# Gates for three batches at a time, alternating half signs and a padded third layer in the mixing stage of a fused transformer block

## The chip, the cores and the metric

The kernel runs on one core of one Trainium2 chip. It is written in Bass and Tile: a Python program emits instructions for the engines PE (TensorE, matrix products), ACT (ScalarE, activations), DVE (VectorE), POOL (GpSimd) and SP (SyncE, which here only issues transfers). Each engine works through its own queue in order, and engines wait for one another by semaphores. The metric is the device time of one execution in microseconds (us). Before the change three runs took 1777.57, 1782.65 and 1783.18 us; their median is 1782.65.

## The reference

The input `x` is 8 batches of 256 rows of 256 features in fp32. Three blocks follow one another, each with a residual and a layer norm behind it:

1. `x = LN(x + attn(x))`: six layers of causal linear attention (16 heads) and a feed-forward net, 256 to 1024 to 256.
2. `x = LN(x + xattn(x, ctx))`: differential cross attention. Each of 16 heads has two softmaxes, from two pairs of projections, and the second is subtracted with a weight `gain`. The heads' outputs are normalized and multiplied by `wo`.
3. `x = LN(x + ffn(x))`: the mixing stage, which the change is mostly about:

```python
gf = _global_net(x.mean(axis=1, keepdims=True))      # 256 -> 128 -> 64 -> 1, one number per batch
out = x
for _ in range(3):                                    # the three cycles
    tf = _coupling_net(out)                           # 256 -> 256 -> 128 -> 64 -> 1, one number per row
    combined = 0.7 * gf + 0.3 * tf
    coupling = 0.1 + adaptive_range * (combined - 0.5) * 2.0
    out = out + coupling * _twist(out)
return out
```

`_twist` splits a row into four quarters `o_r, o_i, p_r, p_i` and returns `[p_r, -p_i, -o_r, o_i]`. Both nets use the exact gelu between their layers and a sigmoid at the end, which the kernel computes as a tanh of half the argument.

## The kernel before, in words

All eight batches stay in the core's memory, a batch as two tiles of 128 rows by 256 features (`xr[b]`). The program is a list of tasks, one per batch and stage (`stage_q`, `stage_s`, `stage_w`, `stage_f` for the attention layers; `setup_u`, `stage_u`, `stage_u2`, `stage_xo` for cross attention; `stage_pre`, `stage_ff` for mixing). Each task is a generator that yields due times, and `run_tasks` always resumes the task that is due first (`NOW[0]` is the due time that it has reached). So the order in which instructions are emitted is a plan made of due times. On PE that order is kept by force: `mm` and `tp` (a product, and a transpose as a product with the identity, all under lines 138 and 143) chain each instruction behind the one before it. `table_op` does the same for those ACT instructions that need a function table (exp, gelu, tanh). Every other instruction is placed in its engine's queue by the scheduler, which follows emission order but lets an instruction whose operands come earlier go first.

Products accumulate in PSUM banks, which are handed out in turn from the pools `p_q` (four), `p_h` (two), `p_o` (one) and `p_av` (one). In cross attention `PU(kind)` picks the pool by the kind of work, in the mixing stage `PF()` goes round `q h q q h q o`.

**Cross attention, about 1383 to 1652 us.** It consists of 32 passes: eight batches, two halves of the heads, two halves of each half. `stage_u` makes the scores once for their row maxima (L836, tile `nm`), and these maxima ride along in the second scores product, which `stage_u2` makes: eight products, each followed by an exp on ACT (L867, whose outputs lie in the buffers `a`, `wraw`, `hl` and `avs`). Sixteen narrow products with the values then sum into `p_av`. ACT copies that to memory (L878, `qe`), PE transposes the copy (`p_h<-ident,qe`, L143), DVE divides by the row sums (L887 to L892, `rc` and `o`) and POOL subtracts the two softmaxes (L894, `fo`). Emission interleaves passes: the products and exps of the next pass are emitted between a pass's `p_av` and its transposes. After every fourth pass `stage_xo` normalizes the heads' outputs (square on ACT L905), transposes them, copies them on ACT (L920, `hl`), multiplies by `wo` (`p_h<-w2h,hl`), adds to the residual (DVE, L928) and normalizes (`normalize2`, whose last step on ACT is L338).

**The mixing stage, about 1653 to 1776 us.** `start_ff` negates one quarter of each batch. Three batches have a head start in `stage_pre`, late in cross attention. `stage_ff(b, cyc)` then runs for three cycles of eight batches, due `FFP` = 3.1 apart; the offsets `F_O` are the due times inside it. A batch of a cycle is: four transposes; a cast on ACT (L1050, `wah`) and the rest on DVE (L1055, `wal`), which split the fp32 value into two parts of the reduced type fp32r; a first layer of 256 by 256 as three fp32r products per tile (`mm3`: high times high, high times low, low times high); two gelus (L1066, `hf`); a split on DVE and POOL (L1076, L1077, `hh` and `hl`); a second layer to 128; a gelu (L1089); a split (L1098 on DVE, L1099 on POOL or DVE); a third layer to 64 columns, three fp32r products; a gelu (L1108); a fourth layer to one number (`f_w,a`, 64 rows deep); a tanh (L1124, `cp`); two activations that make the coefficients for the two halves, with opposite signs (L1126); and four updates on DVE, two per row tile (L1134). In cycle 2 the first layer is split, the second and third are single fp32 products on unsplit weights (tile `num`) and values. Cycle 2 ends with the residual, the last normalization and the store.

In cycle 0 a batch also computes its gate, alone: row sums by DVE (L1003, `osm` in `stage_pre`, `gsum` in `stage_ff`), four products with the first gate weight (`osm,rb` or `gsum,rb`, one column), gelu (L1072), a product to 64, gelu, a product of the broadcast weight, tanh (L1113) and two `base` activations (L1116). The weights of the mixing stage are loaded and split by `prep_mix`, whose work falls into cross attention; `prep_ffn` loads the small ones early.

Of the kernel before, what the change touches and what calls it, by code (L numbers as in the profile page):

```python
# [52 lines left out]
FFP = 3.1  # L53
F_O = (1.45, 2.0, 2.85, 7.6, 11.4, 14.5)
# [39 lines left out]
def decoder_kernel(ctx: ExitStack, tc: tile.TileContext, A, out, nlay=NLAY, groups=GROUPS):  # L94
# [8 lines left out]
    def C(name, shape, dt=F32):  # L103
        return cpool.tile(list(shape), dt, name=name)
# [625 lines left out]
    def PU(kind):  # L730

        if kind == "v":
            return PS("av")
        if NOW[0] < T_END:
            return PS("q")
        if kind == "1":
            return PS("qqo"[turn("1", 3)])
        return PS("q" if kind == "2" else "h")

    wide = []  # L740
# [110 lines left out]
    def stage_u2(b, c, hh, u):  # L851

        tq, tk = stq[u % SD], stk[u % SD]
        if u % 4 == 0:
            xst[b]["oc"] = T2("fo", 2)
        oc = xst[b]["oc"]
        va = xst[b][c][2]
        es = []
        for k in range(2):
            for h in range(4):  # L860
                t = (4 * k + h) * UH / 8
                yield us(t)
                ps = PU("2")
                mm(flat(ps), lhsT=tk[0:98, h, half(k)], rhs=flat(tq[0:98, 2 * h:2 * h + 2, :]), start=True, stop=True)
                yield us(t + 0.5)
                e = ET()
                table_op(act.activation(e, ps, AF.Exp))  # L867
                es.append(e)
        yield us(t + U_O[1])
        po = PU("v")  # L870
        for k in range(2):
            for h in range(4):
                mm(flat(po[32 * h:32 * h + 32]), lhsT=va[:, k, 4 * hh + h, :], rhs=flat(es[4 * k + h]),
                   start=k == 0, stop=k == 1, tile_position=(0, 32 * h))
        t += U_O[1]
        yield us(t + 1.4)
        ov = T2("qe", 2)
        act.copy(ov, po)  # L878
        yield us(t + 2.2)
        pt = PU("x")  # L880
        for mp in range(2):
            for s in range(2):
                tp(pt[:, mp, half(s)], ov[:, mp, half(s)], ident)
        yield us(t + 2.9)
        p5 = pt.rearrange("p m (s h n) -> p m s h n", s=2, h=4)
        rc = S("rc", [P, 2, 2, 4], bufs=2)
        dve.reciprocal(rc, p5[:, :, :, :, 16])  # L887
        dve.tensor_scalar(rc[:, 1], rc[:, 1], gain, None, ALU.mult)
        c0 = (8 * c + 4 * hh) * 16
        og = oc[:, :, c0:c0 + 64].rearrange("p s (h n) -> p s h n", h=4)  # L890
        o2 = S("o2", [P, 2, 2, 4, 16], bufs=2)
        dve.tensor_tensor(o2.rearrange("p m s h n -> p (m s) h n"), p5[:, :, :, :, 0:16].rearrange("p m s h n -> p (m s) h n"),  # L892
                          rc.rearrange("p m s h -> p (m s) h").unsqueeze(3).to_broadcast([P, 4, 4, 16]), ALU.mult)
        pool.tensor_tensor(og, o2[:, 0], o2[:, 1], ALU.subtract)  # L894

    def stage_xo(b, X_O):
# [23 lines left out]
        act.copy(oT, pt)  # L920
# [13 lines left out]
    def prep_ffn():  # L934
        def keep(nm, shape, src, parts=P):
            t = C("f_" + nm, [P] + shape)
            load(t[0:parts], src)
            FW[nm] = t[0:parts]
# [4 lines left out]
        keep("w4", [1], A["L0_ffn_cn_w4"], 64)  # L943
# [4 lines left out]
        keep("cb3", [1], col(A["L0_ffn_cn_b3"]), 64)  # L948
# [6 lines left out]
        ars = C("f_ars", [P, 6])  # L955
        for i, x in enumerate((0.3, -0.3, 0.7, -0.7)):
            dve.tensor_scalar(ars[:, i:i + 1], FW["ar"], x, None, ALU.mult)
        pool.memset(ars[:, 4:5], 0.1)
        pool.memset(ars[:, 5:6], -0.1)
        FW["ars"] = ars  # L960

    def prep_mix():

        raw = [T2("hf", 3), T2("num", 1, F32R).bitcast(F32)]
        sp.dma_start(out=raw[0], in_=A["L0_ffn_cn_w1"].rearrange("(k p) n -> p k n", p=P))
        r2 = raw[1][:, :, 0:P]
        r3 = raw[1][:, 0, P:P + 64]
        sp.dma_start(out=r2, in_=A["L0_ffn_cn_w2"].rearrange("(k p) n -> p k n", p=P))
        sp.dma_start(out=r3, in_=A["L0_ffn_cn_w3"])
# [6 lines left out]
        h2, l2 = T2("xTh", 2, F32R), T2("xTl", 2, F32R)  # L976
        yield 1.1
        for h, x in ((hi, raw[0]), (h2[:, :, 0:P], r2), (h2[:, 0, P:P + 64], r3)):
            dve.tensor_copy(h, x)
        yield 1.2  # L980
        for l, h, x in ((lo, hi, raw[0]), (l2[:, :, 0:P], h2[:, :, 0:P], r2), (l2[:, 0, P:P + 64], h2[:, 0, P:P + 64], r3)):
            pool.tensor_tensor(l, x, h, ALU.subtract)
        FW.update(c1=(hi, lo), c2=(h2[:, :, 0:P], l2[:, :, 0:P]), c3=(h2[:, 0, P:P + 64], l2[:, 0, P:P + 64]), g1=g1, r2=r2, r3=r3)
# [6 lines left out]
    def first_layer(xh, xl, ps):  # L990

        ch, cl = FW["c1"]
        for m in range(2):
            mm3(ps[m], [(ch[:, c, half(m)], cl[:, c, half(m)]) for c in range(2)], [(xh[:, c, :], xl[:, c, :]) for c in range(2)])
            yield m
# [6 lines left out]
    def feature_sums(pt, sm):  # L1002
        dve.tensor_reduce(sm, pt, AX.X, ALU.add)  # L1003
        return sm

    def stage_pre(b, deep):
# [11 lines left out]
        if "sums" not in FW:  # L1018
            FW["sums"] = S("osm", [P, 16], bufs=1)
        i = order.index(b)  # L1020
        sm = feature_sums(pt, FW["sums"][:, 2 * i:2 * i + 2])
# [7 lines left out]
        fst[b]["pre"] = (xh, xl, sm, ps)  # L1029

    def stage_ff(b, cyc):
# [8 lines left out]
        if pre:  # L1040
            xh, xl, sm, ps = pre
        else:
# [8 lines left out]
            if cyc == 2:  # L1051
                pool.tensor_tensor(xr[b], xr[b], o, ALU.add)
                d["xo"] = xr[b]
            yield us(F_O[1])
            dve.tensor_tensor(xl, pt, xh, ALU.subtract)  # L1055
            if cyc == 0:
                sm = feature_sums(pt, S("gsum", [P, 2], bufs=2))
# [6 lines left out]
        for m in range(2) if done else first_layer(xh, xl, ps):  # L1064
            yield us(F_O[2] + 0.7 + 0.7 * m)
            table_op(act.activation(hf[:, m, :], ps[m], AF.Gelu, bias=FW["cb1"][:, m:m + 1]))  # L1066
        if cyc == 0:
            pg = PF()
            for c in range(2):
                mm(pg[:, 0, 0:1], lhsT=FW["g1"][:, c, :], rhs=sm[:, c:c + 1], start=c == 0, stop=c == 1)  # L1070
            g1 = S("gg1", [P, 1], bufs=3)
            table_op(act.activation(g1, pg[:, 0, 0:1], AF.Gelu, bias=FW["gb1"], scale=1.0 / 256))  # L1072
# [7 lines left out]
        if cyc < 2:  # L1080
            ch, cl = FW["c2"]
            mm3(ps[:, 0, :], [(ch[:, c, :], cl[:, c, :]) for c in range(2)], [(hh[:, c, :], hl[:, c, :]) for c in range(2)])
        else:
            for c in range(2):
                mm(ps[:, 0, :], lhsT=FW["r2"][:, c, :], rhs=hf[:, c, :], start=c == 0, stop=c == 1)
# [4 lines left out]
        if cyc == 0:  # L1090
            pg = PF()
            mm(pg[0:64, 0, 0:1], lhsT=FW["g2"], rhs=g1, start=True, stop=True)
            g2 = S("gg2", [64, 1], bufs=3)
            table_op(act.activation(g2, pg[0:64, 0, 0:1], AF.Gelu, bias=FW["gb2"]))
        yield us(F_O[3] + 1.2)
        if cyc < 2:
            hs = T2("hh", HHB, F32R)
            dve.tensor_copy(hs[:, 0, :], h2)  # L1098
            (dve if pre else pool).tensor_tensor(hs[:, 1, :], h2, hs[:, 0, :], ALU.subtract)  # L1099
        yield us(F_O[4])  # L1100
        ps = PF()
        if cyc < 2:
            mm3(ps[0:64, 0, :], [FW["c3"]], [(hs[:, 0, :], hs[:, 1, :])])
        else:
            mm(ps[0:64, 0, :], lhsT=FW["r3"], rhs=h2, start=True, stop=True)
        yield us(F_O[4] + 0.4)
        h3 = h23[0:64, 1, :]
        table_op(act.activation(h3, ps[0:64, 0, :], AF.Gelu, bias=FW["cb3"]))  # L1108
        if cyc == 0:
            pg = PF()  # L1110
            mm(pg[:, 0, 0:1], lhsT=g2.to_broadcast([64, P]), rhs=FW["g3"], start=True, stop=True)
            gt = S("gt", [P, 1], bufs=2)
            table_op(act.activation(gt, pg[:, 0, 0:1], AF.Tanh, bias=FW["gb3"], scale=0.5))  # L1113
            base = S("base", [P, 2], bufs=8)
            for q in range(2):
                act.activation(base[:, q:q + 1], gt, AF.Identity, bias=FW["ars"][:, 4 + q:5 + q], scale=FW["ars"][:, 2 + q:3 + q])  # L1116
            d["base"] = base
# [7 lines left out]
        for q in (1, 0):  # L1125
            act.activation(cp[:, 2 * q:2 * q + 2], cp[:, 0:2], AF.Identity, bias=d["base"][:, q:q + 1], scale=FW["ars"][:, q:q + 1])  # L1126
# [5 lines left out]
        for t in range(2):  # L1132
            for q in range(2):
                dve.scalar_tensor_tensor(no[:, t, half(q)], o[:, t, half(1 - q)], cp[:, 2 * q + t:2 * q + t + 1], base_o[:, t, half(q)], ALU.mult, ALU.add)  # L1134
        d["o"] = no
        if cyc == 2:
            y = no
            yield us(F_O[5] + 2.2)
            dve.tensor_scalar(y[:, :, q1], y[:, :, q1], -1.0, None, ALU.mult)
# [36 lines left out]
    for i, b in enumerate(order):  # L1176
# [13 lines left out]
        tasks.append((t_end + us(UH + U_XO), 1.0, lambda b=b, i=i: stage_xo(b, X_O[i == len(order) - 1])))  # L1190
    t_f = t_u + us(U_FF)
    for i, t in enumerate((18.0, 11.0, 4.0)):
        tasks.append((t_u - us(t), 1.0, lambda b=order[i], deep=i < 2: stage_pre(b, deep)))
    tasks.append((t_f - 2.9, 1.0, prep_mix))
    for cyc in range(3):
# [64 lines left out]
```

## Time and profile before

The profile is of one execution of the program, which took 1778.4 us by itself, with a span of 1776.6 us and a mean granted PE clock of 0.986.

| stage | from to (us) | length | PE busy | DVE busy | ACT busy |
|---|---|---|---|---|---|
| cross attention | 1383 to 1652 | 269 | 249.24 | 228.16 | 213.74 |
| head of mixing | 1652 to 1664 | 12 | 9.14 | 7.09 | 6.06 |
| cycle 0 | 1664 to 1707 | 43 | 42.89 | 28.33 | 33.68 |
| cycle 1 | 1707 to 1732 | 25 | 24.47 | 24.30 | 21.41 |
| cycle 2 | 1732 to 1760 | 28 | 28.00 | 19.22 | 24.32 |
| tail | 1760 to 1776.6 | 16.6 | 4.59 | 9.21 | 9.87 |

Over the whole span PE is busy for 1697.5 us (96%), DVE for 1292.3, ACT for 1173.5 and POOL for 824.7. The borders of the stages are read from PE's products; neighbouring stages overlap on the other engines.

A line of the timeline gives the start in us, the duration in us, the engine, the line of the program, the operation, output and inputs by the program's tile names, shapes, and how many equal instructions it stands for. What stands in brackets is the idle time of the engine before it and what ended that time. A line of the windows gives, after the stretch and its length, the busy time of PE, of PE's weight loads, of DVE, ACT and POOL, each with the number of instructions in brackets, then the granted clock, the busy share of the transfer engines and their GB/s.

### The profile page before, as it was taken

To read this page: it belongs to the slowest core of one execution; us is meant where nothing else is said; L and a number is where in the kernel's file an instruction comes from. 1 tells how busy PE (TensorE), PEld (TensorE's weight loads), DVE (VectorE), ACT (ScalarE), POOL (GpSimd) and SP (SyncE) were. 2 spreads that over 40 slices of the span, in tenths; PEclk is the share of its full clock that TensorE was granted. 3 is DMA by queue.
4 is the path that set the end of the run, shared out by engine and by line. 5 is a ranking of instruction groups with operands and counts; after the bars stand their busy time and mean duration, and the time that the engine had idled before them with its cause. 6 is when DMAs were issued, how large, how long until landed. Compare 5 with 4: busy or idle time off the path is not lost.

```text
span 1776.6 us, 38400 instructions
## 1 busy us (share of the span) xinstructions
PE 1697.5 (96%) x14992; PEld 1352.7 (76%) x14992; DVE 1292.3 (73%) x2855; ACT 1173.5 (66%) x2297; POOL 824.7 (46%) x1289
## 2 busy tenths in 40 slices
PE   6999999999999999999999999999988899999997
PEld 4688887888878888788888887888776645554795
DVE  5566868667776677776787666777668898887586
ACT  3566665666656666667666665666665788887687
POOL 7333444344433444444344434444566676743263
PEclk9899999999999999999999999999999999999898
DMA  5000001000010000100011001000003354440001
GB/s 153 10 1 2 22 19 49 2 1 22 19 49 1 2 22 29 39 1 1 23 37 42 2 1 37 22 22 2 16 25 95 103 145 115 113 126 25 1 1 48
DMA packets 63262, 64.23 MB, mean 36 GB/s; under 512 B 10261, under 2 KB 56600, under 8 KB 63082
## 3 DMA queue, kind: packets, MB, share of 16 engines
q1 hardware_dynamic: 62058, 61.51, 12.2%
q8 instruction: 118, 1.93, 0.4%
q0 software_dynamic: 1024, 0.28, 0.1%
q14 instruction: 62, 0.51, 0.1%
HBM read 49.67 MB, written 11.81 MB: 35 GB/s over the span
## 4 chain that ended last, share of the span: by engine, by line
PE 71%; DVE 13%; ACT 6%; POOL 5%; issue 3%; DMA 1%; SPq 1%; POOLq 0%; ACTq 0%; DVEq 0%
PE p_q L138 24%; PE p_h L138 18%; PE p_o L138 13%; PE p_av L138 10%; PE p_q L143 4%; PE p_h L143 2%; DVE nm L836 2%; DVE a L505 2%; POOL stk L524 1%; POOL hl L579 1%; DVE hh L576 1%; DVE bst L317 1%; POOL nz L295 1%; ACT hf L596 1%; ACT L451 1%
## 5 line engine op out<-in xcount | busy, mean ns | idle before, releaser
L596 ACT ACTIVATE hf<-p_h,bcol 128x256 f32<-128x256 f32 x384 | 161.4, 475 | 214.3 <-PE p_h L138 213.7
L524 POOL TENSOR_SCALAR_AFFINE_SELECT stk<-stk 128x256 f32<-128x256 f32 x384 | 172.6, 475 | 238.4 <-ACT stk L521 235.1
L579 POOL TENSOR_TENSOR hl<-hf,hh 128x512 fp32r<-128x512 f32 x144 | 195.2, 1356 | 160.7 <-DVE hh L576 132.3
L138 PE MATMUL p_q<-stq,kf 32*128 32x512 f32 (+2 forms) x1664 | 248.7, 521 | 10.2 <-ACT wraw L867 1.9
L521 ACT COPY stk<-p_q 128x512 f32<-128x512 f32 x384 | 198.7, 599 | 84.9 <-PE p_q L138 84.4
L294 POOL TENSOR_SCALAR nv<-bmv 128x2 f32<-128x2 f32 x128 | 34.2, 267 | 324.8 <-DVE bmv L319 307.9
L138 PEld LDWEIGHTS p_o<-w2h,hh 128*128 128x128 f32 x768 | 117.8, 190 | 73.3 <-issue 71.9
L138 PE MATMUL p_h<-xTh,w1h 128*128 128x256 f32 x768 | 168.1, 300 | 1.3 <-DVE xTl L392 1.0
L138 PE MATMUL p_o<-w2h,hh 128*128 128x256 f32 x768 | 167.8, 300 | 0.8 <-DVE xr L614 0.8
L138 PE MATMUL p_h<-xTl,w1h 128*128 128x256 f32 x768 | 154.8, 283 | 0.7 <-DVE xTl L392 0.7
L138 PE MATMUL p_h<-xTh,w1l 128*128 128x256 f32 x768 | 154.6, 283 | 0.0
L138 PE MATMUL p_o<-w2h,hl 128*128 128x256 f32 x768 | 152.1, 279 | 0.0
L138 PE MATMUL p_o<-w2l,hh 128*128 128x256 f32 x768 | 151.7, 279 | 0.0
L505 DVE TENSOR_TENSOR a<-p_q,maskT 128x512 f32<-128x512 f32 x192 | 119.2, 683 | 41.6 <-PE p_q L138 41.6
L836 DVE TENSOR_REDUCE nm<-p_q 128x2 f32<-128x512 f32 x189 | 125.2, 678 | 22.3 <-PE p_q L138 21.8
L345 DVE SCALAR_TENSOR_TENSOR xr<-xr,bmv,gb 128x256 f32<-128x256 f32 x192 | 132.3, 727 | 0.0
L138 PE MATMUL p_av<-stk,vaug 128*17 128x256 f32 x1536 | 126.0, 387 | 5.3 <-POOL stk L524 4.5
L138 PEld LDWEIGHTS p_h<-xTh,w1h 128*128 128x128 f32 x768 | 119.0, 191 | 3.7 <-issue 2.6
L138 PEld LDWEIGHTS p_h<-xTh,w1l 128*128 128x128 f32 x768 | 119.8, 191 | 0.0
L138 PEld LDWEIGHTS p_h<-xTl,w1h 128*128 128x128 f32 x768 | 118.8, 191 | 1.1 <-DVE xTl L392 1.1
L138 PEld LDWEIGHTS p_o<-w2h,hl 128*128 128x128 f32 x768 | 117.2, 189 | 0.0
L138 PEld LDWEIGHTS p_o<-w2l,hh 128*128 128x128 f32 x768 | 117.1, 189 | 0.0
(364 smaller groups left out, 4559.3 us busy)
## 6 DMA issues: line engine op xcount, KB each, us to landing
wraw<-in_L_attn_W_dram SPq DMA_DIRECT2D x48, 256.0 KB
xq<-pc SPq DMA_DIRECT2D x16, 384.0 KB
xk<-pc SPq DMA_DIRECT2D x16, 192.0 KB
stq<-xq SPq DMA_DIRECT2D x16, 192.0 KB
stk<-xq SPq DMA_DIRECT2D x16, 192.0 KB
xr<-in_x_dram SPq DMA_DIRECT2D x8, 256.0 KB
px<-in_x_dram SPq DMA_DIRECT2D x8, 256.0 KB
cx<-in_ctx_dram SPq DMA_DIRECT2D x16, 128.0 KB
```

What stands on the lines that cost most here:

```text
L138: ins = pe.matmul(o, **kw)
L143: ins = pe.transpose(*a)
L294: pool.tensor_scalar(v, var, 1e-5, 1.0, ALU.add, ALU.mult)
L295: pool.tensor_tensor(z, v, mhalf, ALU.pow)
L317: dve.bn_stats(st[:, t, :], y[:, t, :])
L345: dve.scalar_tensor_tensor(y[:, t, :], y[:, t, :], mv[:, t, 0:1], g[:, t, :], ALU.subtract, ALU.mult)
L505: follow("dm", dve.tensor_tensor(a0[g].rearrange("p m (e n) -> p (m e) n", e=2), ps[g].rearrange("p m (e n) -> p (m e) n", e=2), maskT4, A ...
L521: act.copy(a1[g // 2][:, g % 2], ps[g])
L524: pool.affine_select(x, x, [[0, 2], [-1, P]], ALU.is_ge, 0.0, base=0, channel_multiplier=1)
L579: (pool if M_L >> j & 1 else dve).tensor_tensor(hl, hs[j], hh, ALU.subtract)
L596: table_op(act.activation(hf[:, m, :], ps[:, m, :], AF.Gelu, bias=b1col(l, 2 * j + m)))
L836: dve.tensor_reduce(nm[:, s, 2 * h:2 * h + 2], ps, AX.X, ALU.max)
```

## The change

It has five parts.

- **Gates.** `stage_gate(i0, i1)` computes the gates of the batches with the places 0 to 2, 3 to 5, and 6 and 7 together, as columns of one product. The row sums of all batches lie in one tile `osm`. One `base` per batch remains, not two.
- **Signs.** One coefficient per row serves both halves. Instead of a coefficient with the opposite sign, the updates add or subtract by cycle, so the halves of `out` change sign between cycles. In cycle 1 the first layer takes negated weights (`neg`, made once in `prep_mix` by two DVE operations), in cycle 2 the gelu takes a scale of -1, and the residual becomes a subtraction.
- **Third layer.** In all cycles it is one fp32 product with weights padded with zeros from 64 to 128 columns, on the unsplit gelu output. The split before it goes, and the split of its weights in `prep_mix`. The fourth layer is padded to 128 rows.
- **Banks.** After `T_X`, the time at which the last pass ends, `PU` takes banks from `p_q`.
- **Order on ACT.** The copies of `p_av` and of the projection's transposes are wrapped in `table_op`, so they keep their place in the chain of exps and gelus.

```diff
+G_T = 2.1
@@ PU
             return PS("q")
+        if NOW[0] > T_X[0]:
+            return PS("q")
@@ stage_u2
-        act.copy(ov, po)
+        table_op(act.copy(ov, po))
@@ stage_xo
-        act.copy(oT, pt)
+        table_op(act.copy(oT, pt))
@@ prep_ffn
-        keep("w4", [1], A["L0_ffn_cn_w4"], 64)
+        keep("w4", [1], A["L0_ffn_cn_w4"], 64, True)
-        keep("cb3", [1], col(A["L0_ffn_cn_b3"]), 64)
+        keep("cb3", [1], col(A["L0_ffn_cn_b3"]), 64, True)
@@ prep_mix
-        r3 = raw[1][:, 0, P:P + 64]
+        r3 = raw[1][:, 0, P:2 * P]
+        pool.memset(r3[:, 64:P], 0.0)
+        sp.dma_start(out=r3[:, 0:64], in_=A["L0_ffn_cn_w3"])
+        neg = S("pc", [P, 3, 256], F32R, 2)
+        dve.tensor_scalar(neg[:, 0, :], hi[:, 1, :], -1.0, None, ALU.mult)
+        dve.tensor_scalar(neg[:, 1, :], lo[:, 1, :], -1.0, None, ALU.mult)
+    def stage_gate(i0, i1):
+        n = i1 - i0
+        pg = PF()
+        for c in range(2):
+            mm(pg[:, 0, 0:n], lhsT=FW["g1"][:, c, :], rhs=FW["sums"][:, i0:i1, c], start=c == 0, stop=c == 1)
+        yield us(0.4)
+        g1 = S("gg1", [P, 3], bufs=1)[:, 0:n]
+        table_op(act.activation(g1, pg[:, 0, 0:n], AF.Gelu, bias=FW["gb1"], scale=1.0 / 256))
+        yield us(1.6)
...
+        gt = S("gt", [P, 3], bufs=1)[:, 0:n]
+        table_op(act.activation(gt, pg[:, 0, 0:n], AF.Tanh, bias=FW["gb3"], scale=0.5))
+        base = S("base", [P, 3], bufs=3)
+        act.activation(base[:, 0:n], gt, AF.Identity, bias=FW["ars"][:, 2:3], scale=FW["ars"][:, 1:2])
@@ stage_ff
-            table_op(act.activation(hf[:, m, :], ps[m], AF.Gelu, bias=FW["cb1"][:, m:m + 1]))
+            table_op(act.activation(hf[:, m, :], ps[m], AF.Gelu, bias=FW["cb1"][:, m:m + 1], scale=-1.0 if cyc == 2 else 1.0))
-        if cyc < 2:
-            hs = T2("hh", HHB, F32R)
-            dve.tensor_copy(hs[:, 0, :], h2)
-            (dve if pre else pool).tensor_tensor(hs[:, 1, :], h2, hs[:, 0, :], ALU.subtract)
-        if cyc < 2:
-            mm3(ps[0:64, 0, :], [FW["c3"]], [(hs[:, 0, :], hs[:, 1, :])])
-        else:
-            mm(ps[0:64, 0, :], lhsT=FW["r3"], rhs=h2, start=True, stop=True)
+        mm(ps[:, 0, :], lhsT=FW["r3"], rhs=h2, start=True, stop=True)
-        for q in (1, 0):
-            act.activation(cp[:, 2 * q:2 * q + 2], cp[:, 0:2], AF.Identity, bias=d["base"][:, q:q + 1], scale=FW["ars"][:, q:q + 1])
+        act.activation(cp[:, 2:4], cp[:, 0:2], AF.Identity, bias=d["base"], scale=FW["ars"][:, 0:1])
-                dve.scalar_tensor_tensor(no[:, t, half(q)], o[:, t, half(1 - q)], cp[:, 2 * q + t:2 * q + t + 1], base_o[:, t, half(q)], ALU.mult, ALU.add)
+                dve.scalar_tensor_tensor(no[:, t, half(q)], o[:, t, half(1 - q)], cp[:, 2 + t:3 + t], base_o[:, t, half(q)],
+                                         ALU.mult, ALU.subtract if (q == 1) != (cyc == 1) else ALU.add)
@@ the list of tasks
+    T_X[0] = t_end + us(UH)
+    for t, i0, i1 in ((G_T, 0, 3), (5 * FFP + G_T, 3, 6), (7 * FFP + G_T, 6, 8)):
+        tasks.append((t_f + us(t), 1.0, lambda i0=i0, i1=i1: stage_gate(i0, i1)))
```

## The prediction

> **What bounds the kernel now.** I first read the windows by stage: span, and busy time (with instruction counts) of PE, weight loads, DVE, ACT and POOL, then the granted clock and the DMA share.
>
> ```profile
> 1383.00:1652.00 269.00, 249.24 (x1732) 141.51 (x1728) 228.16 (x548) 213.74 (x427) 157.18 (x300) 1.00 0.38 103
> 1652.00:1664.00 12.00, 9.14 (x42) 6.18 (x42) 7.09 (x19) 6.06 (x13) 2.52 (x9) 0.73 0.01 1
> 1664.00:1707.00 43.00, 42.89 (x315) 39.42 (x316) 28.33 (x69) 33.68 (x107) 18.48 (x28) 0.96 0.00 1
> 1707.00:1732.00 25.00, 24.47 (x195) 23.03 (x193) 24.30 (x46) 21.41 (x55) 18.05 (x17) 1.00 0.01 2
> 1732.00:1760.00 28.00, 28.00 (x182) 22.68 (x181) 19.22 (x59) 24.32 (x62) 9.86 (x17) 1.00 0.06 20
> ```
>
> The rows are cross attention, the head of the mixing stage, and its cycles 0, 1 and 2. PE is busy 249.24 of 269 us, 42.89 of 43, 24.47 of 25 and 28 of 28: PE's queue, whose order is written out by hand, sets the time. Only in cycle 1 does another engine come near (DVE, 24.30). The head is a latency chain at a clock of 0.73. So a PE instruction saved in cycles 0 to 2 is time saved, and a wait put into PE's queue in cross attention is time lost unless a gap there swallows it.
>
> Second, the timeline of one regular pass of cross attention (pass 18 of 32; a pass is eight exps of scores, one weighted sum p_av, its copy, and four transposes of that copy):
>
> ```profile
> 1556.91 0.59 ACT L878 COPY qe<-p_av 128x512 f32<-128x512 f32 x1 [0.54 <-PE p_av L138]
> ...
> 1557.39 0.60 ACT L867 ACTIVATE wraw<-p_q 128x512 f32<-128x512 f32 x1
> ...
> 1557.86 0.60 PE L143 MATMUL p_h<-ident,qe 128*128 128x128 f32 x4
> 1557.89 0.59 ACT L867 ACTIVATE hl<-p_q 128x512 f32<-128x512 f32 x1
> ...
> 1558.29 0.38 PE L138 MATMUL p_q<-stq,kf 98*128 98x512 bf16 x1
> ```
>
> ACT copies p_av as soon as it is there (0.54 us idle before), then runs two exps. PE reaches the transposes of the copy at 1557.86, 0.36 after the copy's end, and does not wait. The next score matmul follows them.
>
> Third, pass 13, where that copy comes late behind a normalize:
>
> ```profile
> 1516.88 0.56 ACT L878 COPY qe<-p_av 128x512 f32<-128x512 f32 x1
> ...
> 1517.50 0.55 PE L143 MATMUL p_h<-ident,qe 128*128 128x128 f32 x3 [0.96 <-ACT qe L878]
> ```
>
> The copy ends at 1517.44 and PE starts 0.06 later, having stood 0.96 us.
>
> Fourth, PE alone over one batch of cycle 0, then the head, where ACT's table load and two gelus stand before the last copy:
>
> ```profile
> 1695.44 0.60 PE L138 MATMUL p_h<-f_w,a 64*128 64x1 f32 x4
> 1695.97 0.33 PE L138 MATMUL p_q<-hh,xTh 128*64 128x256 f32 x1
> 1696.14 0.28 PE L138 MATMUL p_q<-hh,xTl 128*64 128x256 f32 x1
> 1696.26 0.28 PE L138 MATMUL p_q<-hh,xTh 128*64 128x256 f32 x1
> ```
>
> ```profile
> 1653.33 1.28 ACT L1066 ACT_TABLE_LOAD   x1
> ...
> 1655.36 0.59 ACT L878 COPY qe<-p_av 128x512 f32<-128x512 f32 x1
> ...
> 1663.79 0.56 PE L138 MATMUL p_q<-hh,xTh 128*128 128x256 f32 x1
> ```
>
> **The change part by part.** I used the order of the instructions of both builds on each queue. Everything is costed against the profiled execution, 1778.4 us (span 1776.6); the median shown is 1782.65, so a difference is carried over to that.
>
> *1. The copy of p_av joins the chain of exps.* In 28 of 32 passes (3 to 30) it now stands behind one more exp. In pass 18 the exp of 1557.39 stays, the copy takes the place of the exp of 1557.89 and ends at about 1558.48, and the transposes start at 1558.54 (the 0.06 of pass 13) instead of 1557.86: 0.68 to 0.69. The exp behind and the score matmul at 1558.29 move by as much. Queued behind the waiting transpose is all of PE; for its scores wait ACT's exps, for its maxima DVE. 18 passes pay 0.69 = 12.4; six passes with the output projection have 0.44 us more PE work in front and pay 0.25 = 1.5; pass 13 pays 0.48, pass 28 1.0, and 29 and 30 nothing (weight products stand in front). Sum 15.4.
>
> How much is carried to the end? PE's gaps that have a releaser are 22 us over 1438 to 1627. Eight waits for ACT's wah copy, 0.39 each, 3.2 in all, can swallow a delay of PE; the waits for maxima and exps cannot, as PE itself feeds them. Passes 12 to 16, with the 0.96 stall, took 33.67 us for 31.80 of PE work, passes 16 to 20 without it 32.46 for 31.62: 1.03 more idle, so carried whole; passes 4 to 8 without it 33.65 for 31.79: nothing carried. I take 12, nearer the first. Low end 4 (a stall of 0.25 in place of 0.69 per regular pass, if other gaps close). High end 18.4: in passes 8, 12, 24 and 28 a pair of normalizes also moves ahead of an exp, up to 0.75 each.
>
> *2. The gates.* Batches in cycle 0 start 4.77 us apart (1689.14, 1693.92, 1698.69) and in cycle 1 3.61: a gate costs PE 1.16, four g1 matmuls in 0.45 and g2, g3 with their changes of tile shape in 0.70. Eight of them, 9.3, become three groups of about 1.25, 3.8: -5.5. ACT issues 12 small gate operations instead of 40 (0.25 to 0.38 us each), hidden behind PE.
>
> New wait: g1 of the groups (3 to 5) and (6, 7) stands shortly behind the last batch's transposes and needs the row sums, which DVE makes after the split: ACT's cast 0.59, DVE's subtraction 0.69, the reduction 0.68, less the PE work in between. About 1.5 each, +3.0 (0 to 4). Behind that wait stands the next first layer.
>
> *3. The third layer.* Three products of 64 columns take 0.41 (1695.97 to 1696.38). No row shows one fp32 product of 128 columns over 256 in cycle 0, but the second layer of cycle 2 has that form: 0.216 per pass, two passes, 0.43. +0.02 for 16 batches. The fourth layer after it, with 64 rows, takes 0.63 with its changes of shape; with 128 rows, as the g1 matmuls, 4 x 0.112 = 0.45: -0.18 for 24 batches. In cycle 2 the 64-column product takes 0.58 and slows the next product by 0.10; both go to 0.43 and nothing: -0.25 for 8. Sum: 16 x -0.16 = -2.5, 8 x -0.43 = -3.4; in cycle 2 PE already waits 0.3 in some batches for ACT's wah, so I count -2.7.
>
> The Trainium skill, "FP8 and Floating Point Precision", section TensorE Precision Notes, speaks against this edit: true fp32 takes four passes through the array. By that rule and the 0.12 of a 256-wide pass I would estimate 0.48 for the product, +0.07 instead of +0.02, 0.8 us over 16 batches. The sum goes by the rows.
>
> *4. Off PE.* DVE's cast of the third layer (0.62) and POOL's or DVE's subtraction (0.76) go from 16 batches, one ACT activation (0.38) from 24. That lengthens no queue, and it loosens DVE's 1716 to 1728 stretch and three late-wal gaps of PE (0.34, 0.51, 0.15): -0.8. Two new 128x256 negations on DVE late in cross attention (nearest row: a cast of that shape, 0.28 to 0.42) lie in DVE's 15% idle time: 0, at most +0.7 without it. The pad's memset on POOL falls into an idle stretch of 1.85 us at 1368.40; SP's queue of 419 DMAs keeps its order and its waits, so nothing is late there: 0, at most +0.3. Swaps among POOL's normalizer steps: 0.
>
> Cycles 0 to 2 then: -5.5 -2.5 -2.7 -0.8 +3.0 = -8.5.
>
> *5. Head and tail.* At the head the copy and the projection's copy now precede the table load, and other banks stop PE from waiting for DVE's o (1.24 us at 1658.38) and xr. In its place PE goes through the first group's gate, two round trips to ACT, before the second layer at 1663.79. I follow the chain: the last exp, copy, projection's copy, square (0.63), load 1.28, gelus 0.26 and 0.42 in turn, cast 0.42: second layer at about 1661.5, 2.3 earlier. The granted clock is 0.5 from 1657.46 for 10.24 us, and what is pulled into that stretch runs at half speed: -1.8 (-4 to 0). At the tail DVE's four updates of the last batch no longer wait in two pairs (second at 1768.44, for the coefficient of 1767.98): -1.0 (-1.8 to 0).
>
> "TensorE: Matmul & The Clock Gate", Part 1 of the Trainium skill, has half clock follow an idle window of about 3.4 us. PE's thin stretch, 1654.4 to 1658.4, fits; by the rule, a head without it would keep full clock, and the half-speed work from 1663.79 to 1667.70 would save an estimated 2 us more. The sum leaves that out.
>
> **Sum.** +12 -8.5 -1.8 -1.0 = +0.7: 1779.1 against the profile, 1783.3 against the median.
>
> **The rivals.**
> - *Faster.* The copy's stall is swallowed at its low end: a late PE lets DVE and ACT catch up, so later gaps close. For it: passes 4 to 8 above. Against: PE is 93% busy. +4 -11.3 = -7.3: 1775.3. It decides for faster from a carried stall below 6.
> - *Slower.* The stall is carried whole and the normalizes add theirs: +18.4 -11.3 = +7.1, 1789.7. For it: passes 12 to 20. It decides from 16.6.
> - *Slower, by the mixing stage.* A three-batch gate stalls PE longer than 1.5, or DVE (24.30 of 25 in cycle 1) keeps the pace: -5 there in place of -11.3, +12 -5 = +7: 1789.6. Against: DVE sheds 0.6 to 1.4 of some 3.5 us per batch.
> - *No effect in PE's queue*, if the added order did nothing: excluded, as the copy is seen one exp later in the build.
>
> **How the numbers follow.** A measurement of this kernel can tell about 0.3%, 5.3 us, from no change. Cancelling, as summed: 0.37. Faster rival 0.31. Slower rivals 0.21 and 0.11. The ends, with part 2's waits at 0 and at 4: 4 -11.5 -4 -1.8 = -13.3, and 18.4 -7.5 +0.7 +0.3 = +11.9, so 1769.4 to 1794.6; all ends together are unlikely, and I give 1771 to 1794. Where cancelling holds, 1779 to 1788.
>
> **What would show it.** In the profile after: waits of PE for ACT qe rise from 1.2 us (two times) to about 15 (over 20 times), and cross attention ends 12 us later. Batches of cycle 0 stand 3.5 to 3.6 apart, of cycle 1 3.45, of cycle 2 3.6; two PE waits for DVE osm of 1 to 2 us. The subtraction and cast of the third layer are gone. I am wrong if qe's waits are there but passes keep their spacing, or if the batches keep 3.6 and 4.0 with DVE or ACT in front of PE.

## The result and the profile after

The changed kernel takes 1786.91 us in the median, the kernel before, measured beside it, 1776.51. The ratio is 1.0052, with a 95% interval of 1.0038 to 1.0066: slower, by about half a percent. The profiled execution has a span of 1786.9 us against 1776.6. I split both at three events: the first `p_av` product of pass 0, that of pass 31, and the end.

| stretch (us) | before | after | difference | predicted |
|---|---|---|---|---|
| start to pass 0 | 1381.3 | 1383.7 | +2.4 | 0 |
| pass 0 to pass 31 | 270.8 | 282.4 | +11.6 | +12 |
| pass 31 to the end (mixing) | 124.5 | 120.8 | -3.7 | -11.3 |
| of it: head, to the first second-layer product | 11.69 | 9.17 | -2.5 | -1.8 |
| of it: cycle 0, to the start of its last fourth layer | 44.41 | 47.67 | +3.3 | -3.8 |
| of it: cycle 1 | 30.49 | 29.41 | -1.1 | -2.0 |
| of it: cycle 2 | 26.67 | 23.47 | -3.2 | -2.7 |
| of it: tail | 11.24 | 11.07 | -0.2 | -1.0 |

The first row is no part of the change: over the ten profiles of this study that stretch lies between 1375.6 and 1384.8, and it does not follow the edits. A start of 2.4 us more in one pair of profiles is therefore within what this stretch does anyway.

The windows of the changed kernel, stage by stage as before (span, then PE, weight loads, DVE, ACT, POOL, and the granted clock):

```profile
1383.70:1666.10 282.40, 256.15 (x1745) 140.53 (x1744) 232.74 (x557) 214.16 (x430) 157.71 (x301) 0.99 0.37 98
1666.10:1675.30 9.20, 6.63 (x42) 4.00 (x41) 5.25 (x16) 6.14 (x13) 0.83 (x2) 1.00 0.01 2
1675.30:1723.00 47.70, 42.31 (x278) 40.05 (x278) 24.93 (x64) 29.28 (x74) 16.03 (x28) 0.86 0.00 1
1723.00:1752.40 29.40, 28.69 (x223) 27.46 (x222) 22.45 (x47) 23.02 (x57) 16.58 (x13) 1.00 0.00 1
1752.40:1775.80 23.40, 21.78 (x149) 19.74 (x147) 17.60 (x65) 20.56 (x53) 7.23 (x17) 0.99 0.14 46
```

The passes have 6.9 us more PE time on record than the 249.24 of before, but over a stretch 13 us longer; the head is short and at full clock; and cycle 0, where PE was busy 42.89 of 43 us, now has 5.4 us idle and a clock of 0.86.

The page of the copy, L882, says who waits for it:

```profile
  PE p_av L139: 4.0, 4
...
  PEld p_h L144: 19.6, 26
  PE p_h L144: 11.7, 20
```

Before, ACT stood 25.0 us in 30 waits for `p_av` before this copy. Now it hardly waits for it, and PE stands idle for the copy before the transposes of 20 passes. Pass 18 shows why, in the timeline:

```profile
1566.73 0.60 ACT L871 ACTIVATE wraw<-p_q 128x512 f32<-128x512 f32 x1 [1.02 <-PE p_q L139]
...
1567.23 0.58 ACT L882 COPY qe<-p_av 128x512 f32<-128x512 f32 x1
...
1567.69 0.62 ACT L871 ACTIVATE hl<-p_q 128x512 f32<-128x512 f32 x1
...
1567.86 0.66 PE L144 MATMUL p_h<-ident,qe 128*128 128x128 f32 x4 [0.50 <-ACT qe L882]
```

The copy stands between two exps, not before them. It ends at 1567.81 and the transposes start 0.05 later, 0.50 us after PE had nothing else to do.

PE's waits from the last sum to the end of cycle 0:

```profile
PE p_q L139 <- DVE hl L1109: 2.3, 1, 2.3
PE p_q L139 <- DVE bmv L320: 2.2, 2, 1.7
PE p_h L139 <- ACT gg L1028: 1.6, 1, 1.6
PE p_o L139 <- DVE osm L1018: 1.4, 1, 1.4
PE p_q L139 <- ACT gg L1034: 0.3, 1, 0.3
```

The 1.7 (put down to `bmv`, which DVE made right behind the row sums) and the 1.4 are the second and the third group of gates waiting for `osm`. The 1.6 and 0.3 are the round trips of the first group at the head. The first line, 2.3, is new and was not in the prediction. It comes from DVE's order:

```profile
1678.55 0.23 DVE L1012 TENSOR_SCALAR xr<-xr 128x128 f32<-128x128 f32 x1 [2.30 <-ACT xr L339]
...
1680.57 0.69 DVE L1093 TENSOR_TENSOR wal<-p_o,wah 128x512 fp32r<-128x512 f32 x1 [0.38 <-ACT wah L1088]
...
1681.18 0.68 DVE L1018 TENSOR_REDUCE osm<-p_o 128x2 f32<-128x512 f32 x1
1681.78 1.45 DVE L1109 TENSOR_TENSOR hl<-hf,hh 128x512 fp32r<-128x512 f32 x2
...
1682.68 0.51 PE L139 MATMUL p_q<-hl,xTh 128*128 128x256 f32 x2 [2.29 <-DVE hl L1109]
```

The split of the second layer of the second batch (`hh`, then `hl`) stands in DVE's queue behind a negation of a batch that is due much later, which waits 2.30 us for ACT's normalize, and then behind the low part and the row sums of batch 3. PE gets `hl` at 1682.68.

In the kernel before, `hh` of the second batch stood ahead of such a negation and `hl` directly behind it, ahead of the low part and the row sums of batch 3:

```profile
1663.84 0.43 DVE L1076 CAST hh<-hf 128x512 fp32r<-128x512 f32 x1
...
1668.82 0.23 DVE L1000 TENSOR_SCALAR xr<-xr 128x128 f32<-128x128 f32 x1 [2.57 <-ACT xr L338]
1668.96 0.69 DVE L1077 TENSOR_TENSOR hl<-hf,hh 128x512 fp32r<-128x512 f32 x1
...
1669.71 0.50 PE L138 MATMUL p_h<-hl,xTh 128*128 128x256 f32 x2
```

PE's product follows 0.11 us after the end of the one ahead of it, so this order cost next to nothing.

In the changed kernel PE runs at half clock after each of the three waits in cycle 0, 2.3, 1.7 and 1.4. Windows of one clock period before and behind each:

```profile
1679.66:1683.08 3.42, 1.13 (x9) 0.92 (x8) 2.97 (x5) 0.62 (x2) 2.08 (x5) 1.00 0.00 0
1683.08:1686.49 3.41, 3.41 (x16) 3.23 (x16) 0.15 (x1) 1.43 (x3) 0.00 (x0) 0.50 0.00 0
1693.32:1696.73 3.41, 1.71 (x14) 1.64 (x14) 1.76 (x6) 1.07 (x5) 1.29 (x4) 1.00 0.00 0
1696.73:1700.14 3.41, 3.41 (x19) 3.17 (x17) 1.41 (x6) 2.41 (x7) 0.00 (x0) 0.50 0.03 7
1703.56:1706.97 3.41, 2.03 (x19) 1.86 (x17) 1.72 (x3) 1.50 (x3) 1.29 (x1) 1.00 0.00 0
1706.97:1710.38 3.41, 3.41 (x15) 3.23 (x15) 1.14 (x4) 1.64 (x5) 0.00 (x0) 0.50 0.00 0
```

In the second, fourth and sixth row PE is busy all the time at a clock of 0.50, so each costs 1.7 us of work, 5.1 together, and one more at 1676.25 costs 1.7. In the kernel before, a single half-clock stretch of 10.24 us lay 6.3 us in the head and 3.9 us in cycle 0, where it cost 1.95. (The changed kernel has one stretch of 3.41 in its passes too, at 1423.7; c1 and c3 below have one about there as well.)

### The profile page after: what moved, and what is told of

It reads as the page before. It is cut to its first block, busy times and chain, and to the rows that moved or that the text cites. A ratio compares the mean times of both kernels' runs of the same rounds, so it can differ in the third digit from the quotient of the medians.

```text
span 1786.9 us, 38187 instructions
## 1 busy us (share of the span) xinstructions
PE 1695.9 (95%) x14936; PEld 1349.6 (76%) x14936; DVE 1283.8 (72%) x2835; ACT 1161.2 (65%) x2245; POOL 816.2 (46%) x1277
## 4 chain that ended last, share of the span: by engine, by line
PE 71%; DVE 12%; ACT 7%; POOL 5%; issue 3%; DMA 1%; SPq 0%; POOLq 0%; ACTq 0%; DVEq 0%
PE p_q L139 25%; PE p_h L139 17%; PE p_o L139 13%; PE p_av L139 10%; PE p_q L144 4%; PE p_h L144 3%; DVE a L506 2%; DVE nm L840 1%; POOL nz L296 1%; POOL hl L580 1%; POOL stk L525 1%; DVE bst L318 1%; DVE hh L577 1%; ACT hf L597 1%; ACT L452 1%
## 5 line engine op out<-in xcount | busy, mean ns | idle before, releaser
L840 DVE TENSOR_REDUCE nm<-p_q 128x2 f32<-128x512 f32 x189 | 125.6, 681 | 29.4 <-PE p_q L139 28.6
L139 PEld LDWEIGHTS p_h<-xTl,w1h 128*128 128x128 f32 x768 | 118.7, 190 | 1.1 <-DVE xTl L393 1.1
L139 PEld LDWEIGHTS p_h<-xTh,w1l 128*128 128x128 f32 x768 | 119.6, 191 | 0.0
```

What stands on the lines that cost most here:

```text
L139: ins = pe.matmul(o, **kw)
L840: dve.tensor_reduce(nm[:, s, 2 * h:2 * h + 2], ps, AX.X, ALU.max)
```

## The experiments

The theory after the two traces: cross attention is longer by the copy's new place; cycle 0 loses its gain to two waits for row sums, to one wait made by DVE's order, and to the half clock that follows. Rivals were named with each run. All figures in the table are from one profile each, in us; the last column is PE's half-clock time in mixing before the tail.

| kernel | passes | mixing | head | cycle 0 | cycle 1 | cycle 2 | half clock |
|---|---|---|---|---|---|---|---|
| before | 270.8 | 124.5 | 11.69 | 44.41 | 30.5 | 26.7 | 10.2 |
| changed | 282.4 | 120.8 | 9.17 | 47.67 | 29.4 | 23.5 | 13.7 |
| e1: copy of p_av free | 275.9 | 120.1 | 9.10 | 47.12 | 29.4 | 23.5 | 13.7 |
| e2: before, that copy chained | 282.7 | 129.9 | 12.19 | 49.31 | 30.5 | 26.5 | 10.2 |
| e3: groups 2 and 3 later | 281.8 | 114.3 | 9.17 | 41.12 | 29.5 | 23.5 | 6.8 |
| e4: before, third layer alone | 271.2 | 119.6 | 10.15 | 44.21 | 29.6 | 24.6 | 3.4 |
| e5: gates 3 to 7 single, later | 282.5 | 118.7 | 9.16 | 45.52 | 29.4 | 23.5 | 6.8 |
| e8: banks undone | 282.6 | 116.2 | 10.38 | 41.90 | 29.4 | 23.4 | 3.4 |
| c1: e1 and e3 together | 272.3 | 116.5 | 9.11 | 43.43 | 29.4 | 23.5 | 10.2 |
| c3: c1 and DVE's order | 271.3 | 111.0 | 9.14 | 37.86 | 29.5 | 23.5 | 6.8 |

**The copy taken out of the chain (e1).**

```diff
-        table_op(act.copy(ov, po))
+        act.copy(ov, po)
```

> The changed kernel, with the copy of p_av taken out of the chain of exps again (the copy of the projection's transposes stays in it). Copy theory: PE's waits for ACT qe fall from 28.9 us back to about 2, the stretch from the first p_av sum to the last falls from 282.4 to 270.8 us (within 1), and the run is about 11.6 us shorter than the changed kernel, which is 0.1 to 0.2% below the kernel before. Rival (the projection's copy, the normalizes that were moved, or the two negations make cross attention longer): the stretch stays above 278.

Measured: 1776.99 us, ratio 1.0005 (0.9984 to 1.0026) to the kernel before. The waits are those of before again:

```profile
  PE p_av L139: 26.7, 29
...
  PEld p_h L144: 1.9, 2
  PE p_h L144: 1.2, 2
```

But the passes are 5.1 us longer than before, where I had expected at most 1. Of these, 3.7 arise between passes 2 and 4, and there the profile has a half-clock stretch of 10.24 us:

```profile
1428.32:1431.73 3.41, 3.41 (x14) 1.37 (x13) 3.11 (x9) 2.65 (x6) 1.96 (x2) 0.50 0.16 42
```

The other runs with this copy free, c1 and c3, have passes of 272.3 and 271.3. So most of the 11.6 is the copy's place; what remains, 0.5 to 1.5, may belong to the projection's copy or to the moved normalizes, and was not taken apart. Some of it need not be theirs: e4, with neither copy chained, is 0.4 longer than before as well.

**The same chain alone in the kernel before (e2).**

```diff
-        act.copy(ov, po)
+        table_op(act.copy(ov, po))
```

> The kernel before, with the copy of p_av chained among the exps and nothing else. Copy theory: the stretch of the 32 passes grows from 270.8 to about 282, the mixing stage stays at 124.5, and the ratio to the kernel before is about 1.0065. Rival: under 1.003.

Measured: 1794.25 us, ratio 1.0109 (1.0079 to 1.0139). The passes grow by 11.9, as they should. The mixing stage was expected to stay and grew by 5.4: at the head PE waits 2.7 for the projection's copy, and in cycle 0 it waits 2.6 and 0.9 for DVE's `hh` and `hl` of the second batch, with 6.8 us of half clock there in place of 3.9. The changed kernel, which chains the projection's copy as well and has other banks, doesn't show the waits for the projection's copy and for `hh`, and has 2.3 for `hl`; which of the two removes them was not taken apart. The trace of e8 below speaks against the banks: it has both copies chained and the old banks, and there PE waits 0.7 for the projection's copy and not at all for the second batch's split. But e8 has the new gates and the new third layer as well.

**The groups of gates later (e3).**

```diff
-    for t, i0, i1 in ((G_T, 0, 3), (5 * FFP + G_T, 3, 6), (7 * FFP + G_T, 6, 8)):
+    for t, i0, i1 in ((G_T, 0, 3), (5 * FFP + 3.6, 3, 6), (7 * FFP + 3.6, 6, 8)):
```

> The changed kernel, with the second and third group of gates due 1.5 later, so that on PE they stand behind the first layer of their last batch. Theory that cycle 0 lost the gain to PE's waits for the row sums and to the half clock that follows them: both waits (1.70 and 1.38 us before osm) vanish or fall below 0.5, the two half-clock stretches at 1696.7 and 1707.0 go with them, and mixing, from the last p_av sum to the end, falls from 120.8 by 3 (waits alone) to 6 (waits and clock). Rival (the clock falls for another reason, or the wait only moves to the next product): under 1.5 shorter.

Measured: 1780.30 us, ratio 1.0023 (1.0005 to 1.0042). PE's waits over the same stretch as above:

```profile
PE p_q L139 <- DVE hl L1109: 2.3, 1, 2.3
PE p_h L139 <- ACT gg L1028: 1.6, 1, 1.6
PE p_q L139 <- DVE bmv L320: 0.5, 1, 0.5
PE p_q L139 <- ACT gg L1034: 0.3, 1, 0.3
```

Both waits for the row sums are gone, the half-clock stretches behind them too, and mixing is 6.5 us shorter: the two waits come to 3.1, so about as much again hangs on the clock. (The `bmv` of this table is a short wait in the head.)

**The third layer alone, in the kernel before (e4).**

```diff
-        keep("w4", [1], A["L0_ffn_cn_w4"], 64)
+        keep("w4", [1], A["L0_ffn_cn_w4"], 64, True)
...
-        if cyc < 2:
-            hs = T2("hh", HHB, F32R)
-            dve.tensor_copy(hs[:, 0, :], h2)
-            (dve if pre else pool).tensor_tensor(hs[:, 1, :], h2, hs[:, 0, :], ALU.subtract)
...
-        if cyc < 2:
-            mm3(ps[0:64, 0, :], [FW["c3"]], [(hs[:, 0, :], hs[:, 1, :])])
-        else:
-            mm(ps[0:64, 0, :], lhsT=FW["r3"], rhs=h2, start=True, stop=True)
+        mm(ps[:, 0, :], lhsT=FW["r3"], rhs=h2, start=True, stop=True)
...
```

> The kernel before, with the padded single fp32 third layer and the padded fourth layer, and nothing else. By the prediction's step 3: batches of cycle 1 start 3.45 instead of 3.61 apart and those of cycle 2 3.61 instead of 4.03, mixing is 5 to 6 us shorter than 124.5, a ratio of 0.997. Rival (fp32 with 128 columns costs more than the fp32r form on PE, or its lack of a split changes nothing as PE is not the bound): mixing within 1.5 of 124.5.

Measured: mixing 119.6, 4.9 shorter, of it 0.9 in cycle 1, 2.1 in cycle 2 and 1.5 in the head. The head's 1.5 is not the layer's: before, 6.3 us of the head ran at half clock, here none did. In cycle 0, where 1.25 was expected, 0.2 came, with two new waits of PE, 0.3 and 0.6. So about 3 of the expected 5 to 6 can be put down to the edit: what cycles 1 and 2 gain, at full clock in both kernels. (In cycle 2 the changed kernel is 1.1 shorter still; which of its other parts does that was not taken apart.) The whole is 1776.75 us with a ratio of 1.0007 (0.9986 to 1.0027): this excludes the 0.997 that was expected and shows no gain, though it leaves room for 2.5 us. The ten executions had a mean granted clock of 0.984, the 25 of the kernel before beside them 0.986, which works against e4; how much of the gain that hides is open.

**Banks of the kernel before (e8).**

```diff
-    T_X[0] = t_end + us(UH)
+    T_X[0] = 1e9
```

> The changed kernel with the bank choice of the kernel before at the head. If the banks shortened the head (9.17 us from the last p_av sum to the second layer of the first batch, before 11.69), it goes back to about 11; if the order of ACT did (the copies ahead of the table load), it stays within 0.6 of 9.17.

One execution, 1783.91 us. The head goes back by 1.2 of the 2.5, so the banks bring about half of its gain. That the order on ACT brings the rest is not shown: the head of the kernel before ran 6.3 us at half clock, and in e4, which chains neither copy and has no half clock there, it is 1.5 shorter than that. Cycle 0, however, is 5.8 us *shorter* without the new banks: the 2.3 us wait for `hl` isn't there, and one half-clock stretch before the tail is left where there were four. In this build DVE's queue has the whole split of the second batch ahead of the negation that waits:

```profile
1676.79 0.43 DVE L1108 CAST hh<-hf 128x512 fp32r<-128x512 f32 x1
1677.25 0.69 DVE L1109 TENSOR_TENSOR hl<-hf,hh 128x512 fp32r<-128x512 f32 x1
1681.07 0.23 DVE L1012 TENSOR_SCALAR xr<-xr 128x128 f32<-128x128 f32 x1 [3.13 <-ACT xr L339]
```

The choice of banks at the head decided the order on DVE behind it. Other waits of PE stand in its place (0.8 for `wah`, 0.6 for `wal`), so most of the 5.8 is the clock: 3.1 us of cycle 0 at half clock in place of 13.7, which is 5.3 us of work. The two waits for row sums are still there (1.6 and 1.4), but in this execution no half clock followed them.

**Gates one by one (e5).**

```diff
-    for t, i0, i1 in ((G_T, 0, 3), (5 * FFP + G_T, 3, 6), (7 * FFP + G_T, 6, 8)):
+    for t, i0, i1 in ((G_T, 0, 3),) + tuple((i * FFP + 3.6, i, i + 1) for i in range(3, 8)):
...
```

The lines left out give the gates' small tiles more buffers.

> The changed kernel with gates of batches 3 to 7 one by one, each due 1.5 later than the groups of the changed kernel, so that none waits for its row sums; compare with the run whose groups are due 1.5 later. Five gates in place of two on PE cost 3 x 1.16 = 3.5 us by the prediction's step 2, so cycle 0, from the second layer of the first batch to the last fourth layer, takes 44.6 instead of 41.1. Rival (grouping saves little, the gain is all in the place of the gates): under 1.

One execution, 1783.94 us. Cycle 0 takes 45.52 against 41.12 with the groups in e3: three more gates on PE cost 4.4, near the 3.5 expected; 0.4 of it is a wait for `wal` that e3 doesn't have. Both have 6.8 us of half clock in cycle 0, so it isn't the clock. Grouping the gates is worth what the prediction said; the place of the groups took it away.

**Both cures (c1), and DVE's order (c3).** c1 is e1 and e3 together. c3 adds, in `start_ff` and `stage_ff`:

```diff
-        dve.tensor_scalar(xr[b][:, :, q1], xr[b][:, :, q1], -1.0, None, ALU.mult)
+        follow("d0", dve.tensor_scalar(xr[b][:, :, q1], xr[b][:, :, q1], -1.0, None, ALU.mult))
...
-            dve.tensor_copy(hh, hf)
-            (dve if pre else pool).tensor_tensor(hl, hf, hh, ALU.subtract)
+            i0 = dve.tensor_copy(hh, hf)
+            i1 = (dve if pre else pool).tensor_tensor(hl, hf, hh, ALU.subtract)
+            if pre:
+                follow("d0", i0)
+                follow("d0", i1)
```

> The changed kernel with both cures: the copy of p_av out of the chain, the second and third group of gates due 1.5 later. If the two losses are independent, the stretch of the passes is 271 to 272.5 (where no half-clock stretch falls into it) and mixing, from the last p_av sum on, 110 to 111: about 17 us less than the changed kernel, a ratio of 0.994 to the kernel before. If they share a cause (the copy's place also sets how the mixing stage starts), mixing stays above 114.

> As the run with both cures, and on DVE the splits of the second layer of the three batches with a head start are chained ahead of the negations of the later batches (the row sums and the low part of batch 3 come after them, too). Theory: PE's wait of 2.3 to 2.6 us in the second layer of the second batch is DVE's order, a negation of a later batch that waits for ACT's normalize; then that wait falls below 1, the half-clock stretch behind it goes, and mixing is 2.5 to 4.5 shorter than with both cures alone. Rival (the gelus before the split are late, so the wait only gets another name): under 1.

c1: 1770.30 us, ratio 0.9964 (0.9950 to 0.9978). The passes are in the range; mixing, at 116.5, is not. By the sign named beforehand, above 114, the two losses are not wholly independent, and the waits show how: with the copy free, PE waits longer for DVE at the start of cycle 0, 2.5 for `hh` and 0.7 for `hl` here and 1.9 and 1.1 in e1, against the 2.3 of the changed kernel and e3. Behind the wait stand 6.8 us of half clock. c3: 1762.61 us, ratio 0.9911 (0.9885 to 0.9937), faster than both kernels. DVE now splits the second batch before the negations:

```profile
1662.19 0.42 DVE L1108 CAST hh<-hf 128x512 fp32r<-128x512 f32 x1
1662.65 0.69 DVE L1109 TENSOR_TENSOR hl<-hf,hh 128x512 fp32r<-128x512 f32 x1
1663.26 0.26 DVE L1012 TENSOR_SCALAR xr<-xr 128x128 f32<-128x128 f32 x1
```

and PE's waits from the last sum over the whole of cycle 0 are

```profile
PE p_h L139 <- ACT gg L1028: 1.6, 1, 1.6
PE p_q L139 <- ACT gg L1034: 0.3, 1, 0.3
PE p_q L139 <- DVE bmv L320: 0.3, 1, 0.3
PE p_q L139 <- DVE wal L1093: 0.2, 1, 0.2
```

Cycle 0 is 37.86: 5.6 shorter than in c1, more than the 2.5 to 4.5 expected. The wait is gone (3.2 us), and of half clock cycle 0 has only the 5.3 us that are left of the stretch that begins in the head, against 10.2 in c1: 2.4 us of work. What stays are the round trips of the first group, 1.6 and 0.3.

## Why the prediction came out as it did

The time lies in the stated range (1771 to 1794), but the likeliest case was "no change", 1783.3 on a median of 1782.65, +0.04%. Measured is +0.52%, with the sign of the two slower rivals, which had 0.32 together. That 1786.91 is near 1783.3 is partly luck: the kernel before, measured beside it, had a median 6.1 us below the one that the prediction started from, so the difference is +10.4 us where +0.7 was summed up, and in the two profiles 2.4 of the difference lies ahead of pass 0.

- *Step 1, the copy, was right.* Its stalls were to sum to 15.4 us over 26 passes. The profile after has 26 waits for `qe`; counted from start to start, beyond the spacing where nothing waits, they come to 16.2 us. Carried to the end were to be 12; the passes are 11.6 longer, and e2 alone gives 11.9. What swallows most of the rest is what was named: by the same count, PE's gaps for ACT's `wah` fall from 3.1 us to 0.4.
- *Step 2, the gates, was right in both its terms.* The waits for the row sums were put at 1.5 each: 1.7 and 1.4. Grouping was put at 1.16 per gate saved: by e5 it is 1.5, or 1.3 without the wait for `wal`. The half clock behind the waits is not in the step.
- *Step 3, the third layer, was right in the sum for one batch and wrong in its parts.* Batches of cycle 1 stand 3.43 to 3.44 apart where nothing waits, against 3.45 predicted. On PE, after:

```profile
1719.51 0.50 PE L139 MATMUL p_o<-f_w,a 128*128 128x1 f32 x4
1719.87 0.68 PE L139 MATMUL p_q<-a,num 128*128 128x256 f32 x2
1720.20 0.47 PE L139 MATMUL p_h<-wah,xTh 128*128 128x256 f32 x1
1720.50 0.28 PE L139 MATMUL p_h<-wah,pc 128*128 128x256 f32 x1
```

The product takes 0.33 to the next start, not 0.43, but the product behind it takes 0.30 instead of 0.12: 0.51 together, against 0.41 for the three products of before. The Trainium skill's rule of four passes ("FP8 and Floating Point Precision", TensorE Precision Notes), which the prediction set aside for a row, gave an estimate of 0.48 and stands nearer. The fourth layer makes up for it, with 0.36 against 0.53, and the last two products of the second layer in front of it, behind which the shape no longer changes, take 0.23 against 0.33. Over a whole cycle less comes out, as e4 shows: in cycle 1 only some batches keep 3.45.
- *Step 4 failed.* It costed the edits off PE at nothing or a gain, and said that a lighter DVE loosens PE's waits. DVE got lighter and PE's wait for it longer: 2.3 us, because the order in DVE's queue changed at the start of cycle 0; c3, which sets that order, has no such wait. The order of instructions had been read for PE and ACT; DVE's at that place was not followed. That the three late-`wal` gaps of cycle 1 would go was wrong too: they are still there, 0.4 each from start to start, and cycle 1 is 1.1 shorter in place of 2.0.
- *The clock was costed only at the head (step 5).* That was the larger miss: the prediction's waits in cycle 0 had no clock behind them. Four half-clock stretches instead of one cost 6.8 us of work instead of 1.95 behind the head, 4.9 more. With the 2.3 of DVE that is 7.2, and cycle 0 missed its forecast by 7.1. The prediction held that PE's thin stretch at the head fits an idle window. It does not: from 1654.05 to 1657.46, the 3.41 us before the half clock, PE was busy 1.61. So a window with work and a wait in it was followed by half clock in the profile before already.
- *Step 5, head and tail*: -2.5 instead of -1.8, and -0.2 instead of -1.0.

Of the rivals, "slower, by the mixing stage" is the one that came true in its size: it was put at +7 us, and passes and mixing together give +7.9 in the traces. Its mechanism came true only in part, so the size is in part luck. The gates stalled PE for 3.1 us, about the 3.0 of the sum and not longer; DVE held PE up by its order and not by its pace; and the largest term, 4.9 us of half clock, was in no rival.

## What to carry to other kernels

A wait that is put into the queue of the engine that sets the time costs most of its length (16.2 us of waits for the copy, and passes 11.6 longer), and on PE here it can bring a period of 3.41 us at half clock, which costs 1.7 more; place a small latency chain (the gates) behind the next piece of independent work, not right behind what feeds it. When a change moves instructions, follow the order of *every* queue at the place where they move, also where the engine is getting less work: a cheap operation that waits for another engine blocks all that stands behind it. And take a change of several parts apart: two of the five here pay (the grouping, and the third layer by the profiles of cycles 1 and 2), one (the chain on the `p_av` copy) costs more than these bring, and c3 cures the losses without giving up the gains. The signs and the chain on the projection's copy were not run by themselves.

## What the runs showed of the hardware

Half clock here did not need a period without work. The rows above have PE busy 1.13, 1.71 and 2.03 us of the 3.41 before a stretch at 0.50, that is, 33 to 60%, and each time a stretch follows that lasts 3.41. The Trainium skill ("TensorE: Matmul & The Clock Gate", Part 1) speaks of half clock after at least one idle window of about 3.4 us. The length of the period agrees, 3.41 or a multiple of it in all these profiles; the condition does not, as a window with a wait of 1.4 to 2.3 us in it was enough here; in e8, waits of 1.6 and 1.4 at the same places, in windows with PE busy 2.05 and 2.04, had no such stretch behind them. The waits that the copy makes in cross attention, 0.5 us in 17 passes and 0.9 to 1.1 in three, were followed by no half-clock stretch between 1427 and 1676 us. In e1 a stretch of 10.24 us followed a window in which PE was busy 2.13 of 3.41; the same place in the kernel before, with 2.07 of 3.40, was followed by none. What decides in these cases stays open. One profile can thus differ from another by some us without a cause in the instructions: e1 and c1 differ in the gates of the mixing stage alone, every engine has the same instructions in the same order in their passes, and these take 275.9 and 272.3.

The mean granted clock of whole executions was 0.986 in the kernel before (25 of them), 0.982 in the changed kernel (18), 0.981 to 0.984 in e1 to e4 and c1, and 0.987 in c3 (4).
